# Transposing the normalized input on VectorE instead of TensorE, and issuing small parameter loads later

## The chip, the cores and the metric

The kernel runs on one core of a Trainium2 chip. The core has five engines with their own instruction queues: TensorE (PE, matrix products; PEld is its weight load), VectorE (DVE), ScalarE (ACT), GpSimd (POOL) and SyncE (SP), which here issues most DMAs. The metric is the device time of one execution in microseconds (us).

## The reference

The input is `x` with shape (4, 1024, 512): 4 sequences of 1024 tokens with 512 features. Everything is fp32 unless said otherwise.

```
xn = layernorm(x)                                    # no scale, no shift

# attention: a time-mix with a linear recurrence
xx = concatenate([xn[:, 1:2], xn[:, :-1]], axis=1) - xn   # the token before, minus this one
k  = (xn + xx * time_mix_k) @ Wk.T                   # hidden size 704
r  = (xn + xx * time_mix_r) @ Wr.T
w  = exp(-exp(time_decay))
state_t = state_(t-1) * w + relu(k_t);  o_t = state_t * r_t
a  = layernorm(o @ Wv.T) * ln_gamma + ln_beta

# FFN: 512 -> 2048 -> 512, with roundings to fp16
d  = gelu(xn.astype(fp16) @ W0.T + bias0).astype(fp16)
e  = (d @ W1.T + bias1).astype(fp16)

out = x + a + e
```

Both branches read the same `xn`.

## The kernel before

The tokens are cut into eight blocks of 512 (`TB`), two for each sequence, in order. A block has `NS` = 4 pieces of 128 tokens, and the features have `NC` = 4 pieces of 128. The products need `xn` with features on the partitions, so each block is transposed once. Its transposed form lives in `xnT`, one buffer for the whole kernel, of 128 partitions x 4 feature pieces x 513 columns; column 0 holds the token before the block.

A block `i` goes through these stages:

- `attention(i, xk)`: for each of six hidden pieces the products `pk` and `pr` (L265) on PE, relu on ScalarE (L250), the recurrence as a scan on VectorE (L252), and the product of both, `g` (L276).
- `ffn(i, xf, between)`: 16 steps `n`. `up(n)` makes 128 of the 2048 hidden features (`pd`, L353, eight matmuls, since each weight is split into a high and a low part `w0h`, `w0l`), gelu to fp16 on ScalarE (L361), and a cast on VectorE to `d` (L363). `down(n)` adds their share to four PSUM tiles `pe` (L369, eight matmuls). `up` runs two steps ahead of `down`. In block 0 the second weight is split as it arrives (L119 on ScalarE, L120 on VectorE); later blocks load the split form again (L143).
- Work for other stages is put into the FFN loop through the dictionary `between`: before step 0 the output product of this block's attention with its layernorm and the residual (`attention_out`, L300 to L325), before step 6 the layernorm of the next block's `x` (`next_norm`), before step 10 the transposes and mixed inputs of the next block (`next_inputs`).
- `finish(i, zs, pe)` adds the FFN's result and writes the block out (L391 to L393).

Block 0 has a start of its own, `first_transposed`, in which each piece of 128 tokens is normalized and transposed as soon as it has landed.

`transposed` (L185) makes the next block's transposes on PE, 16 of 128x128, four into each of four PSUM tiles `pt` that come out of the same four-buffer pool as `pd`. `mixed_inputs` (L210) then copies each `pt` into `xnT` (ScalarE, L218), casts it to fp16 as `x16` for the FFN (ScalarE, L222), takes the difference to the token before (`xx`, VectorE, L228), and makes `xk` and, in place, the r-input in `xnT` (VectorE, L230).

The order on each engine's queue is not the program's. It is made when the kernel is built: among the operations that are ready, the one earlier in the program goes first, and a tile's buffer is waited for. On the chip the order is then fixed.

The four pieces of `x` in a block are four tiles in a four-buffer pool, loaded by SP (L80). At the start SP issues the four `x` loads of block 0, then the four pieces of `wk` (L105), the four of `wr` (L107), and from there the larger weights `w0raw` (L132). Five small loads are issued by ScalarE (L93 to L100): the two mixing vectors, the decays in two parts (`w_sb`, on which ScalarE then takes two exponentials), and `bias0`.

Of the kernel before, what the change touches and what calls it, by code (L numbers as in the profile page):

```python
# [9 lines left out]
F32 = mybir.dt.float32  # L10
# [4 lines left out]
P = 128  # L15
# [4 lines left out]
def time_mix_and_gelu_ffn(  # L20
# [26 lines left out]
    nc = tc.nc  # L47
    B, T, C = x.shape
    HID = wkT.shape[1]
    N = w0T.shape[1]  # L50
    TB = 512
    NS = TB // P
    NC = C // P
    NN = N // P


    NF = HID // P
    H0 = NF * P
    HF = P // 2
# [3 lines left out]
    def pool(name, bufs, **kw):  # L63
        return ctx.enter_context(tc.tile_pool(name=name, bufs=bufs, **kw))

    const = pool("const", 1)
    one = pool("one", 1)
    two = pool("two", 2)
    three = pool("three", 3)
    four = pool("four", 4)  # L70
    ps_mm = pool("ps_mm", 4, space=bass.MemoryType.PSUM)
# [2 lines left out]

    def load_x(i):
        b, t0 = blocks[i]
        tiles = []
        for s in range(NS):
            t = four.tile([P, C], F32, tag="x", name=f"x_{i}_{s}")
            nc.sync.dma_start(t, x[b, t0 + s * P : t0 + (s + 1) * P, :])  # L80
            tiles.append(t)
        return tiles


    x_now = load_x(0)
    ident = const.tile([P, P], F32, name="ident")
    make_identity(nc, ident)
# [2 lines left out]

    mk_sb = const.tile([P, NC], F32, name="mk_sb")
    mr_sb = const.tile([P, NC], F32, name="mr_sb")
    nc.scalar.dma_start(mk_sb, mix_k.rearrange("(c p) -> p c", p=P))  # L93
    nc.scalar.dma_start(mr_sb, mix_r.rearrange("(c p) -> p c", p=P))
    w_sb = const.tile([P, NF + 1], F32, name="w_sb")
    nc.vector.memset(w_sb, 0.0)
    nc.scalar.dma_start(w_sb[:, :NF], decay[:H0].rearrange("(c p) -> p c", p=P))
    nc.scalar.dma_start(w_sb[:HF, NF:], decay[H0:].rearrange("(c p) -> p c", p=HF))
    b0_sb = const.tile([P, NN], F32, name="b0_sb")
    nc.scalar.dma_start(b0_sb, bias0.rearrange("(c p) -> p c", p=P))  # L100

    wk_sb = [const.tile([P, HID], F32, name=f"wk_{c}") for c in range(NC)]
    wr_sb = [const.tile([P, HID], F32, name=f"wr_{c}") for c in range(NC)]
    for c in range(NC):
        nc.sync.dma_start(wk_sb[c], wkT[c * P : (c + 1) * P, :])  # L105
    for c in range(NC):
        nc.sync.dma_start(wr_sb[c], wrT[c * P : (c + 1) * P, :])  # L107


    nc.scalar.activation(w_sb, w_sb, AF.Exp)  # L110
# [14 lines left out]

    w1_dram = [dram.tile([P, 2, C], F32R, name=f"w1d_{n}") for n in range(NN)]

# [7 lines left out]
    def load_w1(i, n):  # L135
        w1 = three.tile([P, 2, C], F32R, tag="w1", name=f"w1_{i}_{n}")
        if i == 0:
            raw = three.tile([P, C], F32, tag="raw", name=f"w1raw_{n}")
            nc.sync.dma_start(raw, w1T[n * P : (n + 1) * P, :])
            split(w1[:, 0, :], w1[:, 1, :], raw)  # L140
            nc.sync.dma_start(w1_dram[n].bitcast(F32), w1.bitcast(F32))
        else:
            nc.sync.dma_start(w1.bitcast(F32), w1_dram[n].bitcast(F32))  # L143
        return w1
# [11 lines left out]
    xnT = const.tile([P, NC, TB + 1], F32, name="xnT")  # L156
# [3 lines left out]
    def rstd_of(var, name):  # L160

        n = var.shape[1]
        r = two.tile([P, n], F32, tag=f"rstd{n}", name=name)
        nc.gpsimd.tensor_scalar_add(r, var, EPS)  # L164
        nc.gpsimd.tensor_tensor(r, r, nhalf[:, :n], ALU.pow)
        return r

    def stats_of(mv, s, src, name):
        st6 = two.tile([P, 6], F32, tag="st6", name=name)
        nc.vector.bn_stats(st6, src)  # L170
        nc.vector.bn_aggr(mv[:, s, :], st6)  # L171

    def normalize(dst, src, mean, rstd):
        nc.vector.tensor_scalar(dst, src, mean, rstd, ALU.subtract, ALU.mult)

    def layernorm(i, xs):

        mv = two.tile([P, NS, 2], F32, tag="mv", name=f"mvx_{i}")
        for s in range(NS):
            stats_of(mv, s, xs[s], f"stx_{i}_{s}")  # L180
        rstd = rstd_of(mv[:, :, 1], f"rx_{i}")
        for s in range(NS):
            normalize(xs[s], xs[s], mv[:, s, 0:1], rstd[:, s : s + 1])

    def transposed(i, xn):  # L185

        for c in range(NC):
            pt = ps_mm.tile([P, TB], F32, tag="mm", name=f"pt_{i}_{c}")
            for s in range(NS):
                nc.tensor.transpose(  # L190
                    pt[:, s * P : (s + 1) * P], xn[s][:, c * P : (c + 1) * P], ident
                )
            yield pt

    def first_transposed(xs):


        pts = [ps_e.tile([P, TB], F32, tag="pe", name=f"pt_0_{c}") for c in range(NC)]
        for s in range(NS):
            mv = four.tile([P, 1, 2], F32, tag="mv1", name=f"mvx_0_{s}")  # L200
            stats_of(mv, 0, xs[s], f"stx_0_{s}")
            rstd = rstd_of(mv[:, :, 1], f"rx_0_{s}")
            normalize(xs[s], xs[s], mv[:, 0, 0:1], rstd)
            for c in range(NC):
                nc.tensor.transpose(
                    pts[c][:, s * P : (s + 1) * P], xs[s][:, c * P : (c + 1) * P], ident
                )
        return pts

    def mixed_inputs(i, pts):  # L210

        t0 = blocks[i][1]
        if t0 > 0:
            nc.gpsimd.tensor_copy(xnT[:, :, 0:1], last)
        x16s = []
        xk = one.tile([P, NC, TB], F32, tag="xk", name=f"xk_{i}")
        for c, pt in enumerate(pts):
            nc.scalar.copy(xnT[:, c, 1:], pt)  # L218
            if t0 == 0:
                nc.vector.tensor_copy(xnT[:, c, 0:1], pt[:, 1:2])  # L220
            x16 = four.tile([P, TB], F16, tag="x16", name=f"x16_{i}_{c}")
            nc.scalar.copy(x16, pt)  # L222
            x16s.append(x16)
            if t0 + TB < T:
                nc.gpsimd.tensor_copy(last[:, c, :], xnT[:, c, TB : TB + 1])
            xx = two.tile([P, TB], F32, tag="xx", name=f"xx_{i}_{c}")
            now = xnT[:, c, 1:]
            nc.vector.tensor_sub(xx, xnT[:, c, :TB], now)  # L228
            for dst, m in ((xk[:, c, :], mk_sb), (now, mr_sb)):
                nc.vector.scalar_tensor_tensor(  # L230
                    dst, xx, m[:, c : c + 1], now, ALU.mult, ALU.add
                )
        return x16s, xk
# [109 lines left out]
    def ffn(i, xf, between):  # L343
# [4 lines left out]
        def up(n):  # L348
            pd = ps_mm.tile([P, TB], F32, tag="mm", name=f"pd_{i}_{n}")
            cols = slice(n * P, (n + 1) * P)  # L350
            for c in range(NC):
                for w in (w0h, w0l):
                    nc.tensor.matmul(  # L353
                        pd,
                        w[c][:, cols],
                        xf[:, c, :],
                        start=(c == 0 and w is w0h),
                        stop=(c == NC - 1 and w is w0l),
                    )
            d16 = two.tile([P, TB], F16, tag="d16", name=f"d16_{i}_{n}")  # L360
            nc.scalar.activation(d16, pd, AF.Gelu, bias=b0_sb[:, n : n + 1])  # L361
            d = four.tile([P, TB], F32R, tag="d", name=f"d_{i}_{n}")
            nc.vector.tensor_copy(d, d16)  # L363
            return d

        def down(n, d, w1):
            for s in range(NS):
                for part in range(2):
# [4 lines left out]
                        start=(n == 0 and part == 0),  # L373
                        stop=(n == NN - 1 and part == 1),
                    )

        AHEAD = 2
        waiting = [(up(n), load_w1(i, n)) for n in range(AHEAD)]
        for n in range(NN):
            if n in between:  # L380
                between[n]()
            if n + AHEAD < NN:
                waiting.append((up(n + AHEAD), load_w1(i, n + AHEAD)))
# [8 lines left out]
            nc.vector.tensor_add(zs[s], zs[s], e16)  # L392
            nc.sync.dma_start(out[b, t0 + s * P : t0 + (s + 1) * P, :], zs[s])  # L393

    x16s, xk = mixed_inputs(0, first_transposed(x_now))
    xf = ffn_input(0, x16s)
    for i in range(len(blocks)):
        more = i + 1 < len(blocks)
        state = {}
        gs = attention(i, xk)  # L400
        if i == 0:
            for grp in range(N // W0G):
                load_w0(grp)
            load_late_constants()
        if more:
            x_now = load_x(i + 1)

        def out_stage():
            state["zs"] = attention_out(i, *gs)

        def next_norm():
            layernorm(i + 1, x_now)

        def next_inputs():
            state["mixed"] = mixed_inputs(i + 1, transposed(i + 1, x_now))

        between = {0: out_stage}
        if more:
            between[6] = next_norm
            between[10] = next_inputs  # L420
        pe = ffn(i, xf, between)
        if more:
            x16s, xk = state["mixed"]
            xf = ffn_input(i + 1, x16s)
        finish(i, state["zs"], pe)
# [43 lines left out]
```

## Time and profile before

| what | value |
|---|---|
| median of 3 runs | 975.88 us (974.77 to 976.09) |
| the profiled execution's own time | 976.54 us |
| its span in the trace | 974.8 us |
| mean granted clock of TensorE | 0.997 |
| busy, TensorE / VectorE / ScalarE / GpSimd | 98% / 42% / 17% / 6% |
| PE transposes of blocks 1 to 7 (L190) | 112 instructions, 13.4 us busy |
| mean rate of all DMAs | 109 GB/s |

The profiler writes down when each instruction began and ended on its engine. From this come the busy time of each engine, groups of like instructions, the idle time before each and what ended it, and the chain of work that ended last, followed back from the last instruction. A line such as `L190 PE MATMUL pt<-ident,x` names the source line, the engine, the operation, what is written and what is read. In a timeline the first two columns are the start and the duration in us.

### The profile page before, as it was taken

How to read it: one execution, taken by the hardware profiler on the slowest of the kernel's cores; microseconds unless marked ns; L12 is line 12 of the kernel's file. 1: busy time of each engine (PE TensorE's matmuls, PEld its weight loads, DVE VectorE, ACT ScalarE, POOL GpSimd, SP SyncE). 2: the span in 40 equal slices, each digit the busy share in tenths (PEclk: the TensorE clock that was granted, in tenths of full speed). 3: DMA queues.
4: the chain of work that ended last, by engine and by line, in shares of the span. 5: the costliest groups of instructions: out<-in, count | busy, mean ns of one | idle time of the engine just before them, and what ended most of it. 6: DMA issues, size and time to landing. Idle time of an engine off the chain costs nothing.

```text
span 974.8 us, 8873 instructions
## 1 busy us (share of the span) xinstructions
PE 955.9 (98%) x3328; PEld 594.8 (61%) x3328; DVE 410.4 (42%) x730; ACT 170.5 (17%) x276; POOL 55.8 (6%) x136
## 2 busy tenths in 40 slices
PE   5999999999999999999999999999999999999997
PEld 2447864478644885458854588445884458744685
DVE  6646462443424444253443524436144271532512
ACT  3322410013100131001301013010130101301111
POOL 2011000010001000010000100002000020000100
PEclk9999999999999999999999999999999999999999
DMA  9635650045400454004540145302452024410233
GB/s 302 194 130 163 221 200 0 12 140 171 154 0 22 141 171 142 1 32 141 173 130 0 35 160 173 108 1 65 151 171 87 1 87 136 150 60 0 84 133 129
DMA packets 43228, 106.50 MB, mean 109 GB/s; under 512 B 8241, under 2 KB 8241, under 8 KB 43185
## 3 DMA queue, kind: packets, MB, share of 16 engines
q1 hardware_dynamic: 39328, 105.92, 32.8%
q10 hardware_dynamic: 3856, 0.02, 0.2%
q8 instruction: 26, 0.43, 0.2%
q14 instruction: 18, 0.14, 0.0%
HBM read 89.14 MB, written 16.78 MB: 109 GB/s over the span
## 4 chain that ended last, share of the span: by engine, by line
PE 97%; DMA 2%; ACT 0%; DVE 0%; issue 0%; DVEq 0%; ACTq 0%
PE pd L353 25%; PE pe L369 24%; PE po L300 14%; PE pr L265 14%; PE pk L265 14%; PE pkr L265 3%; PE po L310 2%; PE pt L190 1%; DMA w0raw<-in_L_ffn_W 1%; DMA wk<-in_L_attn_Wk 0%; DMA mr_sb<-in_L_attn_time_mix_r 0%; ACT xnT L218 0%; DVE e L391 0%; ACT x L222 0%; DVE z L392 0%
## 5 line engine op out<-in xcount | busy, mean ns | idle before, releaser
L369 PE MATMUL pe<-w,d 128*128 128x512 f32 x1024 | 257.4, 395 | 0.0
L369 PEld LDWEIGHTS pe<-w,d 128*128 128x128 f32 x1024 | 192.5, 188 | 45.9
L353 PE MATMUL pd<-xf,w0h 128*128 128x512 f32 x512 | 206.5, 403 | 0.3
L353 PE MATMUL pd<-xf,w0l 128*128 128x512 f32 x512 | 202.2, 395 | 0.0
L361 ACT ACTIVATE d<-pd,b_sb 128x512 f16<-128x512 f32 x128 | 88.3, 690 | 453.6 <-PE pd L353 453.6
L265 PE MATMUL pk<-xk,wk 128*128 128x512 f32 x320 | 145.0, 595 | 2.1 <-DVE xk L230 2.1
L363 DVE CAST d<-d 128x512 fp32r<-128x512 f16 x128 | 54.3, 426 | 217.2 <-ACT d L361 216.9
L265 PE MATMUL pr<-xnT,wr 128*128 128x512 f32 x320 | 145.4, 595 | 0.0
L300 PE MATMUL po<-wv_sb,g 128*128 128x512 f32 x320 | 140.8, 595 | 0.0
L353 PEld LDWEIGHTS pd<-xf,w0h 128*128 128x128 f32 x512 | 96.1, 188 | 32.1 <-issue 5.9
L353 PEld LDWEIGHTS pd<-xf,w0l 128*128 128x128 f32 x512 | 96.1, 188 | 24.5 <-issue 1.9
L265 PEld LDWEIGHTS pr<-xnT,wr 128*128 128x128 f32 x320 | 60.8, 190 | 77.7 <-issue 75.9
L265 PEld LDWEIGHTS pk<-xk,wk 128*128 128x128 f32 x320 | 61.0, 191 | 76.2 <-issue 72.6
L300 PEld LDWEIGHTS po<-wv_sb,g 128*128 128x128 f32 x320 | 60.1, 190 | 75.7 <-issue 75.0
L250 ACT ACTIVATE rk<-pk 128x512 f32<-128x512 f32 x40 | 23.9, 597 | 242.2 <-PE pk L265 242.2
L252 DVE TENSOR_TENSOR_SCAN st<-w_sb,carry,rk 128x512 f32<-128x512 f32 (+1 forms) x24 | 30.8, 1283 | 70.4 <-ACT rk L250 70.4
L252 DVE TENSOR_TENSOR_SCAN st<-w_sb,rk 128x512 f32<-128x512 f32 (+1 forms) x24 | 29.4, 1223 | 56.3 <-ACT rk L250 56.3
L170 DVE BATCH_NORM_STATS2 sty<-po 128x6 f32<-128x512 f32 x32 | 22.1, 689 | 73.2 <-PE po L310 67.9
L276 DVE TENSOR_TENSOR g<-st,pr 128x512 f32<-128x512 f32 x40 | 27.5, 687 | 53.6 <-PE pr L265 53.6
L164 POOL TENSOR_SCALAR ry<-mvy 128x1 f32<-128x1 f32 x32 | 11.4, 356 | 516.0 <-DVE mvy L171 516.0
L265 PE MATMUL pkr<-xnT,wr 128*64 128x512 f32 x64 | 29.2, 598 | 0.0
L265 PE MATMUL pkr<-xk,wk 128*64 128x512 f32 x64 | 29.2, 598 | 0.0
(48 smaller groups left out, 451.3 us busy)
## 6 DMA issues: line engine op xcount, KB each, us to landing
w<-w1d SPq DMA_DIRECT2D x112, 512.0 KB, 3.3
x<-in_L_attn_x SPq DMA_DIRECT2D x32, 256.0 KB, 3.9
xres<-in_L_attn_x SPq DMA_DIRECT2D x32, 256.0 KB, 2.7
w1d<-w SPq DMA_DIRECT2D x16, 512.0 KB, 2.9
out<-z SPq DMA_DIRECT2D x32, 256.0 KB, 4.5
w0raw<-in_L_ffn_W SPq DMA_DIRECT2D x16, 256.0 KB, 3.8
w1raw<-in_L_ffn_W SPq DMA_DIRECT2D x16, 256.0 KB, 3.3
wk<-in_L_attn_Wk SPq DMA_DIRECT2D x4, 352.0 KB, 5.0
```

The source lines that it names most:

```text
L164: nc.gpsimd.tensor_scalar_add(r, var, EPS)
L170: nc.vector.bn_stats(st6, src)
L250: nc.scalar.activation(rk[:hw], pk, AF.Relu)
L252: nc.vector.tensor_tensor_scan(st[:hw], w_sb[:hw, h : h + 1].to_broadcast([hw, TB]), rk[:hw], 0.0 if t0 == 0 else carry[:hw, h : h + 1], A ...
L265: nc.tensor.matmul(dst, w[c][:, cols], src, start=(c == 0), stop=(c == NC - 1))
L276: nc.vector.tensor_mul(g[:, h, :], st, pr)
L300: nc.tensor.matmul(pos[s], g[:, h, s * P : (s + 1) * P], wv_sb[:, h, :], start=(first and h == 0), stop=(not first and h == NF - 1),)
L310: nc.tensor.matmul(pos[s], gh[rows, s // 2, :], wv_sb[rows, NF, :], start=first, stop=not first)
L353: nc.tensor.matmul(pd, w[c][:, cols], xf[:, c, :], start=(c == 0 and w is w0h), stop=(c == NC - 1 and w is w0l),)
L361: nc.scalar.activation(d16, pd, AF.Gelu, bias=b0_sb[:, n : n + 1])
L363: nc.vector.tensor_copy(d, d16)
L369: nc.tensor.matmul(pe[s], d[:, s * P : (s + 1) * P], w1[:, part, :], start=(n == 0 and part == 0), stop=(n == NN - 1 and part == 1),)
```

## The change

Four things are changed.

1. The transposes of blocks 1 to 7 are made by VectorE. Its transpose turns each square of 32x32 elements. So an instruction takes 32 tokens of every piece (`j`) and 32 features of every feature piece (`i`), that is 32 partitions x 512 elements, and writes them straight into `xnT`; 4 x 4 such instructions do a block. There is no PSUM tile `pt` and no copy L218 any more for these blocks, and `x16` is cast from `xnT`. For this the four pieces of `x` become one tile with one buffer.
2. Block 0 keeps its PE transposes; their four copies into `xnT` move from `mixed_inputs` to the end of `first_transposed`, ahead of all `x16` casts.
3. The norm of the next block moves from FFN step 6 to step 4 of the program, the transposes and mixed inputs from step 10 to step 7.
4. The five small loads go from ScalarE's queue to SP's: the mixing vectors behind `wk_0`, the other three behind all of `wk` and `wr`, whose pieces now alternate.

```diff
     def load_x(i):
         b, t0 = blocks[i]
-        tiles = []
+        xs = one.tile([P, NS, C], F32, tag="x", name=f"x_{i}")
         for s in range(NS):
-            t = four.tile([P, C], F32, tag="x", name=f"x_{i}_{s}")
-            nc.sync.dma_start(t, x[b, t0 + s * P : t0 + (s + 1) * P, :])
-            tiles.append(t)
-        return tiles
+            nc.sync.dma_start(xs[:, s, :], x[b, t0 + s * P : t0 + (s + 1) * P, :])
+        return xs
...
-    nc.scalar.dma_start(mk_sb, mix_k.rearrange("(c p) -> p c", p=P))
-    nc.scalar.dma_start(mr_sb, mix_r.rearrange("(c p) -> p c", p=P))
...
-    nc.scalar.dma_start(w_sb[:, :NF], decay[:H0].rearrange("(c p) -> p c", p=P))
-    nc.scalar.dma_start(w_sb[:HF, NF:], decay[H0:].rearrange("(c p) -> p c", p=HF))
...
-    nc.scalar.dma_start(b0_sb, bias0.rearrange("(c p) -> p c", p=P))
...
     for c in range(NC):
         nc.sync.dma_start(wk_sb[c], wkT[c * P : (c + 1) * P, :])
-    for c in range(NC):
+        if c == 0:
+            nc.sync.dma_start(mk_sb, mix_k.rearrange("(c p) -> p c", p=P))
+            nc.sync.dma_start(mr_sb, mix_r.rearrange("(c p) -> p c", p=P))
         nc.sync.dma_start(wr_sb[c], wrT[c * P : (c + 1) * P, :])
+    nc.sync.dma_start(w_sb[:, :NF], decay[:H0].rearrange("(c p) -> p c", p=P))
+    nc.sync.dma_start(w_sb[:HF, NF:], decay[H0:].rearrange("(c p) -> p c", p=HF))
+    nc.sync.dma_start(b0_sb, bias0.rearrange("(c p) -> p c", p=P))
...
-    def transposed(i, xn):
-
-        for c in range(NC):
-            pt = ps_mm.tile([P, TB], F32, tag="mm", name=f"pt_{i}_{c}")
-            for s in range(NS):
-                nc.tensor.transpose(
-                    pt[:, s * P : (s + 1) * P], xn[s][:, c * P : (c + 1) * P], ident
+    def transposed(xn):
+
+        src = xn.rearrange("p s (c i a) -> p s c i a", c=NC, a=Q)
+        dst = xnT[:, :, 1:].rearrange("p c (s j b) -> p s c j b", s=NS, b=Q)
+        for j in range(P // Q):
+            for i in range(P // Q):
+                nc.vector.transpose(
+                    dst[i * Q : (i + 1) * Q, :, :, j, :],
+                    src[j * Q : (j + 1) * Q, :, :, i, :],
                 )
-            yield pt
...
+        for c, pt in enumerate(pts):
+            nc.scalar.copy(xnT[:, c, 1:], pt)
+
+    def mixed_inputs(i):
...
-        for c, pt in enumerate(pts):
-            nc.scalar.copy(xnT[:, c, 1:], pt)
+        for c in range(NC):
+            now = xnT[:, c, 1:]
             if t0 == 0:
-                nc.vector.tensor_copy(xnT[:, c, 0:1], pt[:, 1:2])
+                nc.vector.tensor_copy(xnT[:, c, 0:1], now[:, 1:2])
             x16 = four.tile([P, TB], F16, tag="x16", name=f"x16_{i}_{c}")
-            nc.scalar.copy(x16, pt)
+            nc.scalar.copy(x16, now)
...
         def next_inputs():
-            state["mixed"] = mixed_inputs(i + 1, transposed(i + 1, x_now))
+            transposed(x_now)
+            state["mixed"] = mixed_inputs(i + 1)
...
-            between[6] = next_norm
-            between[10] = next_inputs
+            between[4] = next_norm
+            between[7] = next_inputs
```

`Q` is 32. The uses of `xs[s]` become `xs[:, s, :]`.

More of the change, by code (lines that the diff above doesn't have):

```diff
@@ L54, in time_mix_and_gelu_ffn @@
     NN = N // P
+    Q = 32
     NF = HID // P
@@ L179, in layernorm @@
         for s in range(NS):
-            stats_of(mv, s, xs[s], f"stx_{i}_{s}")
+            stats_of(mv, s, xs[:, s, :], f"stx_{i}_{s}")
         rstd = rstd_of(mv[:, :, 1], f"rx_{i}")
         for s in range(NS):
-            normalize(xs[s], xs[s], mv[:, s, 0:1], rstd[:, s : s + 1])
-    def transposed(i, xn):
-        for c in range(NC):
-            pt = ps_mm.tile([P, TB], F32, tag="mm", name=f"pt_{i}_{c}")
-            for s in range(NS):
-                nc.tensor.transpose(
-                    pt[:, s * P : (s + 1) * P], xn[s][:, c * P : (c + 1) * P], ident
+            normalize(xs[:, s, :], xs[:, s, :], mv[:, s, 0:1], rstd[:, s : s + 1])
+    def transposed(xn):
[6 more added lines that the diff above has]
+                    src[j * Q : (j + 1) * Q, :, :, i, :],
                 )
-            yield pt
     def first_transposed(xs):
@@ L200, in first_transposed @@
             mv = four.tile([P, 1, 2], F32, tag="mv1", name=f"mvx_0_{s}")
-            stats_of(mv, 0, xs[s], f"stx_0_{s}")
+            stats_of(mv, 0, xs[:, s, :], f"stx_0_{s}")
             rstd = rstd_of(mv[:, :, 1], f"rx_0_{s}")
-            normalize(xs[s], xs[s], mv[:, 0, 0:1], rstd)
+            normalize(xs[:, s, :], xs[:, s, :], mv[:, 0, 0:1], rstd)
             for c in range(NC):
                 nc.tensor.transpose(
-                    pts[c][:, s * P : (s + 1) * P], xs[s][:, c * P : (c + 1) * P], ident
+                    pts[c][:, s * P : (s + 1) * P], xs[:, s, c * P : (c + 1) * P], ident
                 )
-        return pts
-    def mixed_inputs(i, pts):
+        for c, pt in enumerate(pts):
+            nc.scalar.copy(xnT[:, c, 1:], pt)
+    def mixed_inputs(i):
         t0 = blocks[i][1]
@@ L226, in mixed_inputs @@
             xx = two.tile([P, TB], F32, tag="xx", name=f"xx_{i}_{c}")
-            now = xnT[:, c, 1:]
             nc.vector.tensor_sub(xx, xnT[:, c, :TB], now)
@@ L393, in finish @@
             nc.sync.dma_start(out[b, t0 + s * P : t0 + (s + 1) * P, :], zs[s])
-    x16s, xk = mixed_inputs(0, first_transposed(x_now))
+    first_transposed(x_now)
+    x16s, xk = mixed_inputs(0)
     xf = ffn_input(0, x16s)
```

## The prediction

> **What bounds the kernel now.** I read the page from the top: busy time, then the chain of work that ended last, then the timeline of TensorE around the operation to be removed, then VectorE's timeline in the same stretch, and the start last.
>
> ```profile
> PE 955.9 (98%) x3328; PEld 594.8 (61%) x3328; DVE 410.4 (42%) x730; ACT 170.5 (17%) x276; POOL 55.8 (6%) x136
> ...
> PE 97%; DMA 2%; ACT 0%; DVE 0%; issue 0%; DVEq 0%; ACTq 0%
> PE pd L353 25%; PE pe L369 24%; PE po L300 14%; PE pr L265 14%; PE pk L265 14%; PE pkr L265 3%; PE po L310 2%; PE pt L190 1%; DMA w0raw<-in_L_ffn_W 1%; DMA wk<-in_L_attn_Wk 0%; DMA mr_sb<-in_L_attn_time_mix_r 0%; ACT xnT L218 0%; DVE e L391 0%; ACT x L222 0%; DVE z L392 0%
> ```
>
> TensorE (PE) is busy for 98% of the span and is 97% of the chain. The mean granted clock is 0.997. So time that PE no longer spends comes off the end, as long as nothing else becomes late. The PE transposes `pt` L190 are on that chain with 1%. Their exact price is the distance between their neighbours on PE, once after block 0 and once after block 1:
>
> ```profile
> 114.05 2.02 PE L369 MATMUL pe<-w,d 128*128 128x512 f32 x8
> 115.91 1.91 PE L190 MATMUL pt<-ident,x 128*128 128x128 f32 x16
> 117.75 0.50 PE L353 MATMUL pd<-xf,w0h 128*128 128x512 f32 x1
> ```
>
> ```profile
> 233.05 2.02 PE L369 MATMUL pe<-w,d 128*128 128x512 f32 x8
> 234.91 1.91 PE L190 MATMUL pt<-ident,x 128*128 128x128 f32 x16
> 236.58 0.47 PE L369 MATMUL pe<-w,d 128*128 128x512 f32 x1
> 237.16 0.50 PE L353 MATMUL pd<-xf,w0h 128*128 128x512 f32 x1
> ```
>
> The columns are start, duration, engine and line. Sixteen transposes move the next matmul by 117.75 - 115.91 = 1.84 us in the first case. In the second they move it by 237.16 - 234.91 = 2.25 us, less 0.23 for the one `pe` matmul put between: 2.02 us. The extra 0.18 is a wait of `pd` for a PSUM tile that ScalarE's `x16` cast L222 had still to read. It comes where the next block starts a sequence (i = 1, 3, 5).
>
> VectorE has room, but where it lies matters. This is its timeline in block 1 (with what ended the idle time before each line):
>
> ```profile
> 197.85 0.70 DVE L170 BATCH_NORM_STATS2 sty<-po 128x6 f32<-128x512 f32 x1 [0.69 <-PE po L300]
> 198.46 0.68 DVE L170 BATCH_NORM_STATS2 stx<-x 128x6 f32<-128x512 f32 x1
> ...
> 205.96 1.46 DVE L174 TENSOR_SCALAR x<-x,mvx,rx 128x512 f32<-128x512 f32 x3
> 207.88 0.43 DVE L363 CAST d<-d 128x512 fp32r<-128x512 f16 x1 [0.47 <-ACT d L361]
> 211.61 0.43 DVE L363 CAST d<-d 128x512 fp32r<-128x512 f16 x1 [3.30 <-ACT d L361]
> ...
> 236.36 0.69 DVE L228 TENSOR_TENSOR xx<-xnT 128x512 f32<-128x512 f32 x1
> ...
> 244.40 0.76 DVE L363 CAST d<-d 128x512 fp32r<-128x512 f16 x2
> ```
>
> The reader is to see two things. First, the queues do not keep the program's order: the norm stands at step 6 of the FFN (about 220 us), but ran from 198.5 us, right behind the last residual statistic[...]. Second, from 208 to 236 us VectorE does one cast of 0.43 us in each FFN step of 3.73 us, and it waits 3.30 us in between.
>
> [...] No row of this trace shows a VectorE transpose. [...]
>
> **The change part by part.**
>
> *PE transposes removed* from seven block changes (L190, 112 instructions): 4 x 1.84 + 3 x 2.02 = 13.4 us off the chain. The 28 copies `xnT` L218 that followed them (about 0.6 us each on ScalarE, 17% busy) are off the path and count nothing.
>
> *VectorE transposes added*: 16 in each of seven blocks, each of 32 partitions x 512 elements. [...] Neighbouring VectorE operations overlap: two `e` operations of 685 ns take 1.29 us, so the pitch is 0.60; I take a pitch of p = 0.62 us, 9.9 us per block. Bounds: 0.34 (the pitch of the 0.42 us cast) and 1.14[...], for which the scan row (1225 ns for 512 elements) is the nearest; less than nothing is excluded, as they are additional instructions.
>
> Are they hidden? They need the normalized `x` (ready at 207.4 us) and `xnT`, last read by block 1's `pr` products before 175 us, so they can start at 208. Now `next_inputs` stands at step 7, so casts `d_5` to `d_8` go ahead when ready, but `d_9` and later stand behind all transposes and all mixing. The mixing took 236.36 to 244.40 = 8.04 us. From the end of the `d_4` cast: 208.31 + 9.9 + 8.04 + 4 x 0.43 = 228.0, and `d_9` is cast by 228.4. PE needs it when the tenth `down` begins, at 233.05. So 4.6 us are left and PE waits for nothing. In block 0 the weight splits L120 (0.69 us) share VectorE: 90.07 (end of `d_4`) + 9.9 + 8.04 + 4.8 (four casts, some four and a half splits) + 1.1 (the `d_9` cast and its split) = 113.9, needed at 114.05. That just fits; I count nothing, and at most 1 us. The mixed inputs are ready at about 228 instead of 244, 27 us before the next block's `pk` at 255.4.
>
> *Waits added*: ScalarE's four `x16` casts now wait for all 16 transposes, and the gelu L361 queues behind them; SP's four `x` loads of the block after next wait for the same, with `w` loads behind them. Both waits end near 219 us if the queue order was made with about the right duration. A gelu late by a few us is covered by the same slack; the `x` loads went out at 236.5 before and now go earlier.
>
> *Start, small loads moved*:
>
> ```profile
> 0.72 3.91 SPq L80 DMA_DIRECT2D x<-in_L_attn_x  x4
> ...
> 4.68 2.70 SPq L105 DMA_DIRECT2D wk<-in_L_attn_Wk  x4
> ...
> 7.43 1.85 SPq L107 DMA_DIRECT2D wr<-in_L_attn_Wr  x4
> ...
> 8.53 0.69 DVE L170 BATCH_NORM_STATS2 stx<-x 128x6 f32<-128x512 f32 x1 [1.26 <-DMA x<-in_L_attn_x]
> ```
>
> Four `x` issues beside ScalarE's five take 3.91 us; later, four `wr` issues take 1.85. Without that neighbour, and without 3,856 small packets in front, the last `x` piece (8.53) can come up to 2 us sooner, and with it the chain statistics, transposes, mixing. Against that, SP issues five more DMAs (5 x 0.55 = 2.7 us) ahead of `w0raw`; ScalarE's copy of `xnT` now precedes all `x16` casts; and `w_sb`, with its two exponentials on ScalarE's queue, arrives behind all first weights, perhaps near 15 us, wanted by the scan at 24.33. Bounds: 2.5 us gained to 3 us lost; I take 1.0 gained, as the `x` pieces are first on the path and the rest has slack.
>
> *Sum*: 976.54 (the profiled execution's own time; its span is 974.8, so 1.7 lie around it) - 13.4 - 1.0 = 962.1. That execution stood 0.66 above the median of 975.88, so **961.5 us** against the median, 1.5% faster. About 0.2% (2 us) is what a measurement of this kernel can tell from no change.
>
> **The rivals.**
>
> *A (0.69): as worked out*, 959 to 965.
>
> *B (0.09): part of the cover is missing*, for instance because the queue order was made with shorter transposes than the chip's, so that ScalarE's or SP's waiting instructions hold up a gelu or a `w` load. About 1 us per block gives 961.5 + 7 = 968.5; with the start 3 us worse, 972. For it: a fixed order does not adapt. Against: in block 0 VectorE worked 8 us in one piece (117.4 to 125.5) and PE did not wait.
>
> *C (0.18): VectorE's transposes are too long and `d_9` is late*, slower. The wait in blocks 1 to 6 is 16p - 14.6 us each (233.05 less the fixed terms above), in block 0 it is 16p - 10.0. Against a gain of 14.4 the balance turns at p = 1.0 us. At p = 1.14: 6 x 3.6 + 8.2 = 29.8, so 961.5 + 29.8 = 991 us. For it: [...]no row here shows the operation. [...] If the four-dimensional pieces come out as 256 small instructions (the change not doing what it says), even at 0.15 us each, the smallest VectorE row, 38 us per block would end far above 1,000 us; that is the extreme of this case.
>
> *D (0.04): PE's 13 us come back as another wait*, so about 976. Next in line would be `xf`, `xk` or the `w` loads; `xk` was 11 us early, so little speaks for it.
>
> **How the numbers follow.** The prediction is A's centre. The range of 959 to 972 holds A and B and leaves out C and D, about 0.22. Faster: A and B, 0.78. Same: D, 0.04. Slower: C, 0.18.
>
> **What would show it.** Right: no `pt` row with 112 matmuls; a VectorE transpose row with 112 instructions near 0.7 us; PE idle as before; VectorE busy up by some 70 us; the span shorter by 13 to 15 us; no PE weight load waiting for `DVE d L363`. Wrong: a transpose row above 1.0 us with PE waiting for the casts in FFN steps 9 to 11; ScalarE idle on the transposes with gelus behind; or first products that start later than 15.51 us.

## The result and the profile after

The changed kernel takes 961.27 us (median of 5 runs, 960.67 to 962.04), beside 976.09 us for the kernel before on the same chip (5 runs, 974.77 to 977.31). The ratio is 0.9848, with a 95% interval of 0.9833 to 0.9862: 1.5% faster. The profiled execution took 960.67 us with a span of 958.8 us at a mean granted clock of 0.998; before it was 976.54 us with a span of 974.8 us.

These are the page's lines of the kernel after: the span, the busy time of each engine, and the chain that ended last by engine and by line.

```profile
span 958.8 us, 8659 instructions
...
PE 942.3 (98%) x3216; PEld 583.1 (61%) x3216; DVE 488.2 (51%) x842; ACT 156.4 (16%) x248; POOL 57.5 (6%) x136
...
PE 98%; DVE 1%; DMA 0%; issue 0%; SPq 0%; DVEq 0%; ACT 0%
PE pd L353 25%; PE pe L369 25%; PE po L300 14%; PE pk L265 14%; PE pr L265 14%; PE pkr L265 3%; PE po L310 2%; DMA x<-in_L_attn_x 0%; PE pt L205 0%; DVE e L391 0%; DVE stx L169 0%; DVE z L392 0%; SPq L80 0%; DVE xk L230 0%; DVE w L119 0%
```

PE has 112 instructions less and is still busy for 98% of a span that is 16.0 us shorter. `pt` L190 with its 1% of the chain is gone. VectorE (DVE) went from 410.4 to 488.2 us busy, which is 77.8 us more. Almost all of it is one new row, shown with the ScalarE row that now waits for it (the groups of instructions: busy time, mean ns of one, then the idle time ahead of them and its releaser):

```profile
L190 DVE STREAM_TRANSPOSE xnT<-x 32x512 f32<-32x512 f32 x112 | 78.7, 703 | 2.2
...
L223 ACT CAST x<-xnT 128x512 f16<-128x512 f32 x32 | 18.2, 618 | 33.8 <-DVE xnT L190 33.8
```

**Where the 16.0 us came from.** The chain of waits gives the start of `po`, the first product of the attention output, in each block. In the kernel after:

```profile
57.03 8.58 PE po L300 x20
...
174.89 8.58 PE po L300 x20
...
291.92 8.58 PE po L300 x20
```

In the kernel before:

```profile
59.52 8.58 PE po L300 x20
...
178.53 8.58 PE po L300 x20
...
297.71 8.58 PE po L300 x20
```

So the first `po` comes 2.49 us earlier, block 0 is 1.15 us shorter (117.86 instead of 119.01), and block 1 is 2.15 us shorter (117.03 instead of 119.18). The later blocks gain 1.95 and 2.16 in turn. Together the seven block changes give 13.46 us; with the start that is 15.95 of the 16.0 us. The last block ends as before. These are two single profiles. Between the medians lie 14.8 us; the experiments show that it is the start that differs from execution to execution.

### The profile page after: what moved, and what is told of

It reads as the page before. It is cut to its first block, busy times and chain, and to the rows that moved or that the text cites. A ratio compares the mean times of both kernels' runs of the same rounds, so it can differ in the third digit from the quotient of the medians.

```text
span 958.8 us, 8659 instructions
## 1 busy us (share of the span) xinstructions
PE 942.3 (98%) x3216; PEld 583.1 (61%) x3216; DVE 488.2 (51%) x842; ACT 156.4 (16%) x248; POOL 57.5 (6%) x136
## 4 chain that ended last, share of the span: by engine, by line
PE 98%; DVE 1%; DMA 0%; issue 0%; SPq 0%; DVEq 0%; ACT 0%
PE pd L353 25%; PE pe L369 25%; PE po L300 14%; PE pk L265 14%; PE pr L265 14%; PE pkr L265 3%; PE po L310 2%; DMA x<-in_L_attn_x 0%; PE pt L205 0%; DVE e L391 0%; DVE stx L169 0%; DVE z L392 0%; SPq L80 0%; DVE xk L230 0%; DVE w L119 0%
## 5 line engine op out<-in xcount | busy, mean ns | idle before, releaser
L190 DVE STREAM_TRANSPOSE xnT<-x 32x512 f32<-32x512 f32 x112 | 78.7, 703 | 2.2
L163 POOL TENSOR_SCALAR ry<-mvy 128x1 f32<-128x1 f32 x32 | 11.4, 357 | 506.8 <-DVE mvy L170 506.8
L391 DVE TENSOR_TENSOR e<-pe,b_sb 128x512 f16<-128x512 f32 x32 | 20.6, 685 | 19.4 <-PE pe L369 19.4
```

The lines of the kernel that those rows point to most:

```text
L190: nc.vector.transpose(dst[i * Q : (i + 1) * Q, :, :, j, :], src[j * Q : (j + 1) * Q, :, :, i, :],)
L391: nc.vector.tensor_add(e16, pe[s], b1_sb)
```

## Experiments

My theory (T in the expectations) was that the time comes from two independent gains, the PE transposes and the moved loads, and that VectorE's work is hidden by a small margin. Against it stood that the start's gain comes from the order of ScalarE's copies (R1), and that the two moved FFN steps are what lets the work hide (R2). T2 names the slow clock of PE's first products. Each run is compared with runs of the kernel before on the same chip, 976.58, 977.19 and 976.76 us in the three groups.

**Without the moved loads.** The changed kernel, with its small loads and the order of `wk` and `wr` as before:

```diff
-        if c == 0:
-            nc.sync.dma_start(mk_sb, ...)
-            nc.sync.dma_start(mr_sb, ...)
+    nc.scalar.dma_start(mk_sb, ...)      # all five on ScalarE again
```

> The changed kernel, but with the small loads and the order of wk and wr as they were before (ScalarE's queue; four wk, then four wr). Theory T (two separate gains: 13.5 us from PE transposes that are gone, 2.5 us from the earlier start, which comes from moving the small loads): the first steady PE stretch starts again near 20.9 us instead of 18.4, the six full block periods stay at 117.03 us, the time is about 963.8 us. Rival R1 (the earlier start comes from the other order of block 0's copies in ScalarE's queue): stays at about 961.3.

Measured: 962.89 us (962.70 to 963.47), ratio 0.9861 (0.9846 to 0.9876), span 961.2. Its chain of waits:

```profile
59.42 8.58 PE po L300 x20
...
177.27 8.58 PE po L300 x20
...
294.31 8.58 PE po L300 x20
```

The first `po` is back within 0.1 us of before, and the blocks stay at 117.85 and 117.04. So the two gains are separate, and the start's needs the moved loads: the changed order of ScalarE's copies, still there, does not give it. The timelines of SP and VectorE show how. First this run:

```profile
0.72 3.91 SPq L80 DMA_DIRECT2D x<-in_L_attn_x  x4
...
8.55 0.69 DVE L169 BATCH_NORM_STATS2 stx<-x 128x6 f32<-128x512 f32 x1 [1.44 <-DMA x<-in_L_attn_x]
```

Then the changed kernel:

```profile
0.72 1.81 SPq L80 DMA_DIRECT2D x<-in_L_attn_x  x4
...
5.50 0.69 DVE L169 BATCH_NORM_STATS2 stx<-x 128x6 f32<-128x512 f32 x1 [0.36 <-DMA x<-in_L_attn_x]
...
6.33 0.66 DVE L169 BATCH_NORM_STATS2 stx<-x 128x6 f32<-128x512 f32 x1
```

With five issues on ScalarE beside them, of 0.47 to 0.59 us each, the four `x` issues take 3.91 us and VectorE waits 1.44 us for the last piece. Without, they take 1.81 us, and the last statistic starts at 6.33 instead of 8.55. So the issues from a second engine went with a loss of 2.1 us of issue time on the queue that mattered; this run shows the loss, but not whether the issues or the small packets behind them cause it.

**The moved loads alone**, on the kernel before:

> The kernel before, with nothing changed but the small loads and the order of wk and wr. T: the start is 2.5 us earlier, block periods stay at 119.0 and 119.2 us, about 973.5 us. R1: no gain, 976. If the five issues on SP's queue delay the weights of block 0 (rival R3), the gain at the start is given back before block 0's output product begins: 976 or more.

Measured: 975.06 us (973.41 to 976.26, 18 runs), ratio 0.9986 (0.9979 to 0.9993), span 973.4. That is 1.5 us less than before (0.7 to 2.1), where 2.5 were expected. The blocks have the periods of before, as expected, but the first `po` of the profile is at 58.20, 1.32 us earlier. The last statistic starts at 6.97, 1.56 earlier. Then PE's first products ran slowly: the granted clock in the windows from 16 to 18 us was 0.50, weight loads took 0.33 us instead of 0.19, and they came every 0.85 us instead of 0.43. Such a stretch lasts from some 16 to 20 us in the profile of before (clock 0.50 from 17 to 19 us), to 19.2 us here, and is absent in the next run. The changed kernel and the run without the moved loads have it too, by their weight loads (0.34 us until 16.4 and 18.6 us), though their windows give a clock of 1.00 at that time. The length of the stretch varies from profile to profile: from the first product to the first `po` it takes 42.5 or 42.6 us where the stretch is absent, and up to 44.2 us where it is there (two runs below, with a late exponential, apart).

So a single profile's start is uncertain by up to 1.7 us. What comes before the first product is steadier. It starts 7.0 us behind the last statistic in the kernel before, in the changed one, in this run and in the one without the moved loads; the order of ScalarE's copies changes nothing in that. Of the 2.49 us I can therefore tie 2.2 (6.33 against 8.53) to the loads. But the last piece's arrival varies too: the last statistic starts between 5.98 and 6.97 us in six profiles with moved loads, and at 8.53 and 8.55 in the two without. The 1.5 us of this run, a median, are the better price of the loads.

**The moved FFN steps undone**: norm at step 6, transposes and mixing at step 10 again, all else as changed.

```diff
-            between[4] = next_norm
-            between[7] = next_inputs
+            between[6] = next_norm
+            between[10] = next_inputs
```

> The changed kernel with the norm at step 6 and the transposes and mixing at step 10, as before. T (operations that are ready move up, and the norm is held only by the statistics buffer behind the last residual, not by its step): norm and transposes start at the same time, near 201 and 204 us in block 1; as the casts and weight splits of steps 9 to 11 now go ahead of the mixing, block 0's 0.8 us wait for a weight split goes away: 960.5 us. Rival R2 (the moved steps are what makes the transposes fit): the transposes start three steps (11 us) later, the mixed inputs of the next block come late, and each block waits some us: 970 or more.

Measured: 960.04 us (959.05 to 961.74), ratio 0.9833 (0.9820 to 0.9847), span 957.2. In block 1 VectorE does its first transposes at 202.21 us, 28.9 us behind the block's first `po` and in groups of 3, 5, 6 and 2, both as in the changed kernel, and block 1 lasts 117.04. So these positions do not decide where the work runs: it moves up as soon as it is ready. One thing differs. The changed kernel has this in PE's timeline of block 0:

```profile
111.56 0.40 PE L369 MATMUL pe<-w,d 128*128 128x512 f32 x1
112.50 1.90 PE L369 MATMUL pe<-w,d 128*128 128x512 f32 x7 [0.54 <-DVE w L119]
```

The `down` product waits for a split of the second weight that stands behind the transposes and much of the mixing on VectorE. With steps 6 and 10 this wait is gone, and block 0 lasts 117.30 instead of 117.86 us. The 0.27 us that it still has over the other blocks lie within its first `po`, which takes 8.85 us instead of 8.58 in this early start. The rest of the gain is PE's start, which had no slow stretch in this execution.

**Four transposes of a block done twice**, that is 4 x 0.715 = 2.9 us more VectorE work:

```diff
+        pairs = [(j, i) for j in range(P // Q) for i in range(P // Q)]
+        for j, i in pairs + pairs[:4]:
```

> The changed kernel with 4 of each block's 16 VectorE transposes issued a second time (same data). Theory T (VectorE's transposes are free only as far as the casts behind them have slack: 2.9 us in blocks 1 to 6, nothing in block 0, which already waits 0.8 us): 4 x 0.715 = 2.9 us more per block use up the slack of blocks 1 to 6 and show in block 0 alone: 961.3 + 2.9 = 964.2 us. Rival (VectorE has room for them anyway, as it is busy for 51% only): 961.3.

Measured: 965.75 us (964.36 to 966.00), ratio 0.9881 (0.9866 to 0.9896), span 963.8. The chain and PE's waits (us in total, times, longest us):

```profile
59.01 8.58 PE po L300 x20
...
179.88 8.58 PE po L300 x20
...
296.91 8.58 PE po L300 x20
```

```profile
PE pe L369 <- DVE d L363: 3.2, 1, 3.2
```

Block 0 is 3.0 us longer (120.87), block 1 not at all (117.03), and so it goes on. VectorE's added work is free in blocks 1 to 6 and paid in full in block 0. The other 2 us of the difference lie ahead of the first `po`, which starts at 59.01 instead of 57.03; what delays it was not shown.

**Twelve done twice**, 8.6 us more per block:

> The same with 12 of the 16 issued twice. T: 12 x 0.715 = 8.6 us more per block; blocks 1 to 6 wait 8.6 - 2.9 = 5.7 us each, block 0 0.8 + 8.6 = 9.4, together 42 us more than the changed kernel: about 1003 us, and TensorE's weight loads in the FFN wait for VectorE's cast d L363. That is slower than the kernel before, as the prediction's third case had it. Rival (free): 961 to 964.

Measured: 999.05 us (992.85 to 1001.06), ratio 1.0214 (1.0179 to 1.0249), span 996.2. It is slower than the kernel before. PE's waits, and below them the one of block 1 in PE's timeline:

```profile
PE pe L369 <- DVE d L363: 21.6, 7, 4.5
...
PE pe L369 <- DVE w L119: 3.2, 1, 3.2
```

```profile
237.31 3.22 PE L369 MATMUL pe<-w,d 128*128 128x512 f32 x8 [2.21 <-DVE d L363]
```

The wait is the one that rival C named: `down` stands for a cast `d` that is queued behind transposes and mixing. Blocks 1 to 6 are 31.8 us longer together, 5.3 each, and 5.7 were expected. But that agreement is a coincidence. The waits themselves are 2.2 us in blocks 1, 3 and 5 and 4.5 us in 2, 4 and 6, 20.2 us in sum. The other 11.6 us come after them. The windows of PE in block 1 (length, busy time and number of matmuls, granted clock, share and rate of the DMAs):

```profile
233.00:235.00 2.00, 2.00 (x9) 1.00 0.73 203
235.00:237.00 2.00, 0.10 (x1) 1.00 1.00 358
237.00:239.00 2.00, 1.69 (x5) 0.75 0.90 334
239.00:241.00 2.00, 2.00 (x6) 0.50 0.39 158
241.00:243.00 2.00, 2.00 (x9) 0.90 0.65 248
```

After the gap PE runs at half the clock for some 3 us; this is why the eight matmuls shown above take 3.22 us and not 2.02. What comes after the wait is 1.8, 1.6, 0.3, 3.0, 1.8 and 3.1 us in blocks 1 to 6, and the mean granted clock of windows of 120 to 125 us, one for each of these blocks, is 0.99, 0.99, 1.00, 0.97, 0.99 and 0.97. The 0.01 and 0.03 missing are an estimated 1.2 and 3.7 us, which fits to the rounding. So the bill of a late cast was waiting plus a slow clock, and the length of the gap alone does not set the second part: the gaps of blocks 1, 3 and 5 are alike. Of the 8.6 us added, 4 to 6 us were covered; each of these kernels has its own order on VectorE's queue. Block 0 added 5.8 us instead of about 8.6.

**Four `rstd` tiles at the start**, so that the third normalization need not wait for a buffer:

```diff
-        r = two.tile([P, n], F32, tag=f"rstd{n}", name=name)
+        r = (four if n == 1 else two).tile([P, n], F32, tag=f"rstd{n}", name=name)
```

> The changed kernel with four buffers instead of two for the one-column reciprocal deviations, so that in block 0 GpSimd need not wait for the first normalization before it begins the third piece's. T (the start is a chain from the last x piece through statistics, GpSimd, normalization, PE transposes, mixing; each us taken from it comes off the end): the fourth normalization moves from 9.87 to about 8.5 us, the start and the whole are 1.2 us shorter: 960.0 us. Rival: the weights' arrival holds the first products anyway, no change.

Measured: 959.63 us (957.52 to 959.96), ratio 0.9823 (0.9809 to 0.9836), span 957.5. The expected mechanism failed: the first normalization now starts at 7.71 instead of 7.12, behind a wait of 0.85 us for GpSimd (`rx` L164), and the mixing starts at 12.19 instead of 11.79, although the last `x` piece came 0.35 us earlier here. From the last statistic to the first product it is 7.75 us instead of 7.0, so the four tiles cost 0.75 us at the start. Nor did the time come from the start; its first `po` is at 57.89. Blocks 1 to 6 last 116.72 instead of 117.03 us, and the difference is in `down`: eight of its matmuls take 1.845 instead of 1.863 us, with the same order of work on PE in these blocks. That the edit shifts other tiles in memory, and `down` with them, was the author's guess; where tiles lie was not read out.

**Two unused tiles of 128x1**, set to zero at the start, to test that. The tiles are meant to shift other tiles; whether and by how much they did was not measured, and the 8 bytes of the expectation are not shown.

> The changed kernel with two unused tiles of 128x1 set to zero by VectorE at the start, so that tiles allocated after them lie 8 bytes further on each partition; the work on PE and its order are untouched. Theory L (the shorter FFN steps of the run with four rstd tiles came from where the tiles lie): the eight-matmul down product L369 takes 1.845 instead of 1.863 us, a block lasts 116.72 instead of 117.03 us, and the time is 961.3 - 7.6 x 0.31 = 958.9 us. Rival N (they came from GpSimd's order at the start, or from something else): 117.03 us per block stays, 961.3 us.

Measured: 959.86 us (959.65 to 960.27), ratio 0.9831 (0.9817 to 0.9844), span 957.8. Blocks last 116.85 us, between the two expectations. The `down` row of the groups is first that of the changed kernel, then with two unused tiles (lines are three higher), then with four `rstd` tiles:

```profile
L369 PE MATMUL pe<-w,d 128*128 128x512 f32 x1024 | 256.8, 395 | 0.5 <-DVE w L119 0.5
```

```profile
L372 PE MATMUL pe<-w,d 128*128 128x512 f32 x1024 | 255.1, 393 | 0.6 <-DVE w L122 0.6
```

```profile
L369 PE MATMUL pe<-w,d 128*128 128x512 f32 x1024 | 254.5, 393 | 0.7 <-DVE w L119 0.7
```

The same matmuls in the same order are 1.7 and 2.3 us shorter in sum. So an edit that does not touch this work changes `down` by up to 1%. That the placement of tiles is the cause was the author's estimate; no run shows it.

**PE kept busy at the start**, with 24 unused transposes before the first `x` and six behind block 0's, to see whether the slow stretch then stays away:

```diff
+    warm(24, "pw_0")      # nc.tensor.transpose(..., ident, ident)
     first_transposed(x_now)
+    warm(6, "pw_1")
```

> The changed kernel with 24 idle transposes of the identity on TensorE before block 0's transposes and 6 behind them, into a PSUM tile that nothing reads. Theory T2 (the first products ran at half the clock in most executions, weight loads of 0.33 us instead of 0.19[...]; that is what made the start differ by 1 to 2 us between runs): no weight load of 0.33 us among the first products, steady stretch from about 17.4 us instead of 18.4, 960.3 us. Rival: the slow first products are the weights' arrival, and nothing changes, 961.3 us, or the idle transposes delay block 0's own, 962.

Measured: 966.18 us (965.34 to 966.84), ratio 0.9885 (0.9869 to 0.9902): slower than without. ScalarE's timeline shows why:

```profile
11.44 1.07 ACT L209 COPY xnT<-pt 128x512 f32<-128x512 f32 x2 [9.44 <-PE pt L205]
16.32 0.21 ACT L109 ACTIVATE w_sb<-w_sb 128x6 f32<-128x6 f32 x1 [3.80 <-DMA w_sb<-in_L_attn_time_decay]
16.43 0.57 ACT L209 COPY xnT<-pt 128x512 f32<-128x512 f32 x1
```

The edit changed the order on ScalarE's queue: the first exponential of the decays came ahead of the last two copies of `xnT`, waited 3.80 us for its late load, and the first `po` came at 63.18 us. PE stood idle for 4.08 us and was slow after that (weight loads of 0.34 us from 20.0 us on), so the run does not answer the question. What it does show is the price of the moved `w_sb` load when its user stands early in a queue; in the changed kernel the exponential stands behind three `x16` casts and waits 1.14 us, with nothing behind it late.

**All three edits together** (steps 6 and 10, four `rstd` tiles, busy PE) has the same fault:

> The changed kernel with steps 6 and 10 again, four buffers for the one-column reciprocal deviations, and the idle transposes at the start. If the parts add up (0.6 to 0.8 us from block 0's wait, 0.3 us per block seen with the four buffers, 1 us at the start): 957.5 us. If the shorter block period with four buffers was a chance of where the tiles lie: 959.5 us.

Measured: 962.86 us (962.31 to 963.22), ratio 0.9854 (0.9839 to 0.9868), first `po` at 62.76. From there on every block, block 0 too, lasts 116.72 us, so those two edits add up.

**Steps 6 and 10 and four `rstd` tiles**, without the busy start:

> The changed kernel with next_norm back at step 6, next_inputs back at step 10, and four rstd tiles at the start. If the two effects add: block 0 loses its wait for the weight split (117.3 or less instead of 117.9) and each block lasts 116.72 us; the run with rstd tiles alone had a span of 957.5 with 1.17 us lost in block 0, so 956.3 us of span and 958.1 us of time, +-1.1 for how long the first products run at the half clock. If they do not add: 959.6, as the better of the two alone.

Measured: **957.88 us** (957.53 to 958.36), ratio 0.9810 (0.9796 to 0.9823), span 955.6. It is the fastest version, faster than before and than the changed kernel, whose interval (0.9833 to 0.9862) lies above this one. Its chain:

```profile
57.03 8.65 PE po L300 x20
...
173.86 8.58 PE po L300 x20
...
290.58 8.58 PE po L300 x20
```

The first `po` starts as in the changed kernel to 0.01 us, but by chance: the first product comes at 14.49 instead of 13.32 us, mostly the price of the four tiles, and there is no slow stretch behind it. Block 0 lasts 116.83 and block 1 116.72 us.

**The same with a busy PE and late exponentials**, the two exponentials now standing behind the `x16` casts in the program:

> As the run with steps 6 and 10 and four rstd tiles, with 24 unused identity transposes on PE before the first x has landed and 6 behind block 0's transposes, and with ScalarE's two exponentials of the decays placed behind the x16 casts in the program, so that ScalarE does not wait for the decays ahead of the four xnT copies. Theory W [...]: no stretch of weight loads at 0.33 us, and the first po starts at 56.0 us or earlier; 958.1 - 1.0 = 957.1 us. Rival: the half-clock stretch comes whatever PE did before 13 us; 958.1 us, first po at 57 us. If the small transposes themselves hold up block 0's transposes, later than 958.1.

Measured: 958.02 us (957.54 to 958.37), ratio 0.9811 (0.9797 to 0.9824), span 955.6, first `po` in the chain at 57.03. The expected gain did not come, because the run without the unused transposes had no slow stretch to remove: in both, the first two `pk` matmuls start at 14.49 us and the next products follow at the same times. Whether an idle PE makes the stretch stays open.

## Why the prediction was right, point by point

The predicted time was 961.5 us, with the range of 959 to 972; the measured one is 961.27. Both terms of the sum were too small in the profile, and the two covers for VectorE's work were thinner than worked out; in block 0 that shows, with 0.8 us. That the centre is met to 0.2 us is in part luck, as the last point tells.

- **PE transposes removed, 13.4 us.** Measured 13.46 us in the seven block changes, but this is 14.3 less a wait of 0.8 us: an undersized step and a missing wait that cancel. The step was mis-sized by 0.11 to 0.14 us per block: I measured up to the start of the next `pd`, and the first `pd` matmul after the transposes takes 0.34 us to the next one (117.75 to 118.09 in the timeline of before) instead of 0.23. So an undisturbed block change is worth 1.95 or 2.16 us and not 1.84 or 2.02.
- **VectorE transposes, near 0.7 us at a pitch of 0.62.** The profile of before has no such transpose, and nothing in it showed the 0.7 us. The rows after the change are 699 to 709 ns. The pitch does not hold. VectorE's timeline in block 1 after the change:

```profile
203.81 2.13 DVE L190 STREAM_TRANSPOSE xnT<-x 32x512 f32<-32x512 f32 x3
205.97 0.43 DVE L363 CAST d<-d 128x512 fp32r<-128x512 f16 x1
206.43 3.58 DVE L190 STREAM_TRANSPOSE xnT<-x 32x512 f32<-32x512 f32 x5
210.04 0.43 DVE L363 CAST d<-d 128x512 fp32r<-128x512 f16 x1
210.50 4.28 DVE L190 STREAM_TRANSPOSE xnT<-x 32x512 f32<-32x512 f32 x6
...
226.03 0.42 DVE L363 CAST d<-d 128x512 fp32r<-128x512 f16 x1
```

  Three take 2.13, five 3.58 and six 4.28 us: 0.715 us each, no overlap. A block's 16 cost 11.4 us, not 9.9. The step that failed is the carry-over of the overlap from two `e` operations (685 ns each, 1.29 us for both), which start on the same partitions, to instructions that each write other partitions than the one before. Whether the kind of instruction or the partitions prevent the overlap, no run tested. One place hints at the partitions: the first transpose of block 0, from and to partitions 0 to 31, runs from 87.29 to 87.99 us, and the cast behind it starts at 87.93, before its end; the casts behind the other groups start after the end (205.97 after 205.94).
- **Hidden in blocks 1 to 6 with 4.6 us left.** Hidden it is, but with less to spare. The last line above ends at 226.45; it is the cast `d_9`, and the tenth `down` begins at 229.41 on the same timeline, so 3.0 us are left; `d_8`, which the prediction left out, has 2.7 (223.01 to 225.68). Of the missing 1.6 us, the pitch is 1.5: 16 x 0.095. The mixed inputs are ready at 226 us, which looks earlier than the 228 that I gave, but the whole block lies 3.6 us earlier than before (174.89 against 178.53), so they are 1.7 us late. The run with four more transposes a block (2.9 us) left these blocks unchanged (117.03 in block 1); the run with twelve more (8.6 us) did not.
- **Block 0 "just fits", at most 1 us.** It does not quite fit: 0.8 us of its gain are missing, with the wait for the split weight L119. The prediction had this split in its sum, as part of the 1.1 us; the term too small was again the pitch. With 0.715 the sum ends at 115.4 us, 1.4 us late, where 0.8 were measured. Steps 6 and 10 take the wait away.
- **Rival B's mechanism is there, without its price.** The casts wait behind groups of up to six transposes (210.50 to 214.78), up to some 3 us. ScalarE's `x16` casts stand 33.8 us in all for VectorE, and one gelu in block 1 starts behind them at 217.78, 3.1 us later than its step of 3.73 us would have it. PE felt none of it. This fits a queue order made with shorter transposes than the chip's, but no run tested that.
- **Rival C** is the real limit of this design. Its formula 16p - 14.6 per block, with the work of twelve more put in as p = 28 x 0.715 / 16 = 1.25, gives 5.4 us, and 5.3 were measured on average. But only 3.4 of these are waits, so the term for the wait was too large, and a term for the slow clock after a gap was missing. Its premise, a transpose above 1.0 us, did not hold. The 1.14 us of its worst case are an estimate that agrees with the scan row, 1225 ns, less the 0.085 us by which two `e` operations overlap.
- **Start, 1.0 us gained.** Measured 2.49 in the profile, near the upper bound, and 1.5 in the run with the loads alone. About 2.2 of the 2.49 are the earlier last `x` piece, which I had put at up to 2 us and then cut by half for risks. Of these risks the late `w_sb` did cost ScalarE a wait (1.14 us), off the path. The remaining 0.3 us go with PE's slow first products, which vary from profile to profile.
- The two errors of size, 1.5 us too little for the start and 0.1 too little for the blocks, explain the span: 974.8 - 13.4 - 1.0 = 960.4 against 958.8. The runs of the changed kernel have their median 0.6 us above its profiled one, so the medians agree more closely than the sums. Their difference is 14.8 us, against 14.4 predicted: 13.4 of it in the blocks leave 1.4 for the start. So the 1.0 was not far off for a usual execution, and the 2.49 belong to the fastest of the five runs. The prediction had also moved its result by 0.66 us for the place of one execution of before among its runs; that this did no harm is luck.

## What to carry to other kernels

Where PE is on the chain for 98% of the time, as here, work of another engine that takes something off PE pays by PE's own pitch, including the slower first matmul behind it: 1.95 or 2.16 us for the 16 transposes of a block change, in which the first `pd` matmul behind them has 0.34 us to the next one instead of 0.23. What it may cost is read from one number: the smallest distance between the end of a cast that is queued among or behind the new work and the product that needs it; check that number in the block with the most other work, here block 0. If it is used up, PE loses the wait and, where the clock is low behind the gap, a slow stretch after it: with twelve more transposes, 2.2 to 4.5 us of waiting in a block and 0.3 to 3.1 us after it. Small loads that start beside the first big ones can delay them: four `x` issues took 3.91 us beside five small ones and 1.81 us without. A late load is harmless only while its user stands late in its own queue: the wait for `w_sb` was 1.14 us off the path in the changed kernel, and 3.80 us on it in the run with the busy PE.

## What the runs showed of the hardware

- VectorE transposes of 32x512 fp32, each to other partitions than the one before, did not overlap one another: 703 ns each, 0.715 us apart, while two `e` operations of 685 ns take 1.29 us. Their four-dimensional pieces ran as one instruction each.
- Eight products of the same shape, in the same order, took 1.863 or 1.845 us, by edits that only add or move small tiles elsewhere.
- PE's first products at the slow rate (weight loads of 0.33 us instead of 0.19) lasted from 0 to some 4 us in different profiles, and moved the first `po` by up to 1.7 us. In the run with twelve more, the clock behind a gap of 2.2 us in block 1 was 0.50. Eight `down` matmuls behind gaps of that length took 3.22 us in block 1 and 3.41 in block 5, but 2.13 in block 3; without a gap they take 2.02. In the run with four more, behind a gap of 3.2 us, they took 2.50 us at a mean clock of 1.00 over the 14 us around it.
